# A graph-network layer: gathered features copied on ScalarE into the tile that TensorE reads

## The chip, the core and the metric

The kernel runs on one core of a Trainium2 chip. The core has five engines with instruction queues of their own: TensorE (PE, matrix products and transposes; its weight loads are shown apart as PEld), VectorE (DVE), ScalarE (ACT), GpSimd (POOL) and SyncE (SP). They work side by side and wait for one another through semaphores. The DMA engines move data between the chip's memory and the on-chip SBUF; TensorE writes into PSUM. The metric is the device time of one execution, in microseconds (us).

## What is computed

The layer passes messages along 212500 edges of a graph of 12500 nodes with 64 features each, sorted by their destination, and updates every node:

```python
msg_in     = concatenate([nodes[row], nodes[col], edge_features], axis=-1)   # 64 + 64 + 32
messages   = relu(msg_in @ mW1 + mb1) @ mW2 + mb2                            # hidden 128, out 64
aggregated = segment_sum(messages, col, num_segments=12500)
upd_in     = concatenate([nodes, aggregated], axis=-1)
out        = layernorm(x + relu(upd_in @ uW1 + ub1) @ uW2 + ub2)
```

`row` is an edge's source, `col` its destination. All of it is float32.

## The kernel before

The edges are cut into 554 groups of 384 (three tiles of 128 edges, an edge to a partition; the last group has 148). Because the edges are sorted by destination, the destinations of one group lie in a window of 32 consecutive nodes, whose first node is read from the data. A second, unordered version of the kernel stands behind a flag for inputs where this doesn't hold, and is not run here.

For each group g the tile `s` (128 partitions x 3 x 96 float32) holds for every edge 32 columns of a one-hot row (which of the window's nodes is its destination) and 64 columns of its source's features.

- `gather(g)` (L92 to L100): three indirect DMAs on POOL's queue fetch the 64 features of 128 source nodes each into columns 32 to 95 of `s`. The tile comes from a ring of 18 buffers (`AHEAD + 2`), and `gather(g + 16)` is called in iteration g.
- `onehot(g)` (L282 to L287): one DVE instruction compares the node numbers with 0 to 31 and writes columns 0 to 31 of the same `s`.
- `turn(g)` (L290 to L300): three TensorE transposes turn `s` into `xt` in PSUM (96 x 384, two buffers); one ACT instruction copies that into the tile `st` and sums the one-hot columns into `counts` (a second ACT instruction reads the sum out).
- `hidden(g)` (L302 to L315): three products of `st` (which also holds the 32 edge features, loaded by SP) with `wm`, a tile with the window's 32 rows of a per-node table and the weights; one ACT instruction applies relu into `h`.
- `sums(g)` (L317 to L326): a tiny transpose of the counts and three products of `h` with the one-hot columns of `s`, into `sg` in PSUM (two buffers).
- `add(g)` (L328 to L331): DVE adds `sg` to the running sums `agg`, and the counts to a row of `xc`.

`window` (SP) loads the 32 table rows of group g + 4, `inputs` (SP) loads the edge features of four groups at a time, `tables_for` makes the per-node table in 25 chunks ahead of its use, and `step_update` runs the node update of a finished chunk of 512 nodes in four steps, one step to an iteration.

The order of the instructions in each queue is written out by hand: each engine takes its own in the order of the program's calls, and the framework puts in the semaphore waits. The main loop's order in iteration g is

```python
gather(g + AHEAD); tables_for(g + SOON); window(g + NEXT)
onehot(g + 2); turn(g + 1); hidden(g)
sg = sums(g - 2); step_update(g - 2); add(g - 2, sg)
```

So in iteration g TensorE runs the transposes of g + 1, the `pre` products of g and the `sg` products of g - 2; ACT runs the copy to `st` of g + 1 and the relu of g; DVE runs the one-hot of g + 2 and, behind it, the addition of g - 2. An `s` buffer is given back when the `sg` products of its group are done.

Of the kernel before, what the change touches and what calls it, by code (L numbers as in the profile page):

```python
# [10 lines left out]
F32 = mybir.dt.float32  # L11
BF16 = mybir.dt.bfloat16
I32 = mybir.dt.int32
AF = mybir.ActivationFunctionType
# [5 lines left out]
P = 128  # L20
N = 12500
E = 212500
D = 64
# [5 lines left out]
W = 32  # L29
TG = 3  # L30
# [11 lines left out]
def tiles_of(g):  # L42

    n = min(GE, E - g * GE)
    return [min(P, n - j * P) for j in range((n + P - 1) // P)]


def plan():
# [22 lines left out]
def ordered(ctx: ExitStack, tc: tile.TileContext, a, ok):  # L71
# [3 lines left out]
    nc = tc.nc  # L75
    x, out = a["x"], a["out"]
    const = ctx.enter_context(tc.tile_pool(name="const", bufs=1))
    dram = ctx.enter_context(tc.tile_pool(name="dram", bufs=1, space=DRAM))
    gp = ctx.enter_context(tc.tile_pool(name="gather", bufs=AHEAD + 2))
# [11 lines left out]
    gathered = {}  # L91

    def gather(g):
        s = gp.tile([P, TG, W + D], F32, name="s")
        for j, p in enumerate(tiles_of(g)):
            t = g * TG + j
            nc.gpsimd.indirect_dma_start(  # L97
                out=s[:p, j, W:], out_offset=None, in_=x[:, :],
                in_offset=bass.IndirectOffsetOnAxis(ap=src_sb[:p, t : t + 1], axis=0),
            )  # L100
        gathered[g] = s
# [7 lines left out]
    for g in range(AHEAD):  # L109
        gather(g)  # L110
# [7 lines left out]
    iota = iop.tile([P, W], F32, name="iota")  # L118
# [72 lines left out]
    def tables_for(g):  # L191

        while tables and tables[0][3] <= g:
            table()
# [51 lines left out]

    early.close()
    ep = ctx.enter_context(tc.tile_pool(name="edge", bufs=3))
    up = ctx.enter_context(tc.tile_pool(name="upd", bufs=2))
    xtp = ctx.enter_context(tc.tile_pool(name="xt_ps", bufs=2, space=PSUM))  # L250
    prp = ctx.enter_context(tc.tile_pool(name="pre_ps", bufs=2, space=PSUM))
    sgp = ctx.enter_context(tc.tile_pool(name="sg_ps", bufs=2, space=PSUM))
    counts = const.tile([D + W, G], F32, name="counts")

    st, starts, hs = {}, {}, {}

    def inputs(b):
        if b * SB >= G:
            return
        c0, c1 = b * SB * GE, min(E, (b + 1) * SB * GE)  # L260
        t = stp.tile([P, SB * GE], F32, name="st")
        nc.sync.dma_start(t[D + W :, : c1 - c0], a["efT"][:, c0:c1])
        st[b] = t

    def columns(g):
        t, c = st[g // SB], (g % SB) * GE
        return t, c, sum(tiles_of(g))

    def window(g):
        if g >= G:  # L270
            return
        if g % SB == 0:
            n = min(SB, G - g)
            _, v = nc.values_load_multi_w_load_instructions(
                start_i[0:1, g : g + n], engines=[ET.SP, ET.DVE], min_val=0, max_val=N - 1,
                skip_runtime_bounds_check_because="they were clamped to the nodes on the chip",
            )
            for i in range(n):
                starts[g + i] = v[i]
        nc.sync.dma_start(wm[g % NW][:W, :], by_dst[bass.ds(starts[g], W), :])  # L280

    def onehot(g):  # L282
        if g >= G:
            return
        nc.vector.tensor_tensor(  # L285
            gathered[g][:, :, :W], iota.unsqueeze(1).to_broadcast([P, TG, W]),
            dlc[:, g * TG : (g + 1) * TG].unsqueeze(2).to_broadcast([P, TG, W]), ALU.is_equal,  # L287
        )

    def turn(g):  # L290

        if g >= G:
            return
        s = gathered[g]
        t, c, n = columns(g)
        xt = xtp.tile([D + W, GE], F32, name="xt")
        for j, p in enumerate(tiles_of(g)):
            nc.tensor.transpose(xt[:, j * P : j * P + p], s[:p, j, :], ident[:p, :p])  # L298
        nc.scalar.activation(t[: D + W, c : c + n], xt[:, :n], AF.Copy,  # L299
                             accum_out=counts[:, g : g + 1])  # L300

    def hidden(g):  # L302
        t, c, n = columns(g)
        sizes = tiles_of(g)
        pre = prp.tile([P, TG, H], F32, name="pre")
        for j, p in enumerate(sizes):
            nc.tensor.matmul(pre[:p, j, :], t[:, c + j * P : c + j * P + p], wm[g % NW],  # L307
                             start=True, stop=True)
        h = ep.tile([P, TG, H], F32, name="h")
        if len(set(sizes)) == 1:  # L310
            nc.scalar.activation(h, pre, AF.Relu)  # L311
        else:
            for j, p in enumerate(sizes):
                nc.scalar.activation(h[:p, j, :], pre[:p, j, :], AF.Relu)
        hs[g] = h  # L315

    def sums(g):  # L317
        h, s = hs.pop(g), gathered.pop(g)
        sizes = tiles_of(g)
        sg = sgp.tile([P, TIMES + 1, W], F32, name="sg")  # L320
        nc.tensor.transpose(sg[0:1, TIMES, :], counts[:W, g : g + 1], ident[:W, :W])  # L321
        for j, p in enumerate(sizes):
            nc.tensor.matmul(sg[:, :TIMES, :], h[:p, j, :],  # L323
                             s[:p, j, :W].unsqueeze(1).to_broadcast([p, TIMES, W]),
                             start=j == 0, stop=j == len(sizes) - 1)
        return sg  # L326

    def add(g, sg):  # L328
        at = bass.ds(starts.pop(g), W)
        nc.vector.tensor_tensor(agg[:, at], sg[:, 0, :], agg[:, at], ALU.add)  # L330
        nc.vector.tensor_tensor(xc[0:1, at], sg[0:1, TIMES, :], xc[0:1, at], ALU.add)  # L331
# [53 lines left out]
    def step_update(g):  # L385

        nonlocal now
        if not now and waiting and waiting[0][0] <= g:
            steps = waiting.pop(0)[1]
            now = [steps[0](), *steps[1:]]  # L390
        elif now:
            got = now[1](now[0])
            now = [got, *now[2:]] if len(now) > 2 else []
# [2 lines left out]
    inputs(1)  # L396
    for g in range(NEXT):
        window(g)
    onehot(0)
    onehot(1)  # L400
    turn(0)
    for g in range(G + 2):
        if g < G:
            if g % SB == 0:
                inputs(g // SB + 2)
            if g + AHEAD < G:
                gather(g + AHEAD)
            tables_for(g + SOON)
            window(g + NEXT)
            onehot(g + 2)  # L410
            turn(g + 1)
            hidden(g)
        if g > 1:
            sg = sums(g - 2)
            step_update(g - 2)
            add(g - 2, sg)
# [284 lines left out]
@with_exitstack  # L701
def gnn_layer(ctx: ExitStack, tc: tile.TileContext, a):
    nc = tc.nc
    flag = ctx.enter_context(tc.tile_pool(name="flag", bufs=1))
    ok = flag.tile([1, 1], I32, name="ok")
    with tc.manual_schedule():
        ordered(tc, a, ok)
    good = nc.values_load(ok[0:1, 0:1], min_val=0, max_val=1,
                          skip_runtime_bounds_check_because="a comparison's result")
    with tc.If(good == 0):  # L710
        with tc.manual_schedule():
            unordered(tc, a)
# [35 lines left out]
```

## Time and profile before

Three runs took 2529.65, 2532.01 and 2534.0 us, median 2532.01. The profiled execution took 2528.93 us; its span, from the first to the last instruction, is 2527.2 us, so 1.7 us lie outside it, and it stands 3 us under the median.

| what | before |
|---|---|
| profiled execution | 2528.93 us |
| span | 2527.2 us |
| TensorE busy (9359 matmul records) | 1697.3 us, 67% |
| POOL busy (1661 indirect DMAs) | 1570.3 us, 62% |
| ACT busy | 598.2 us, 24% |
| DVE busy | 392.9 us, 16% |
| mean granted TensorE clock | 0.786 |

The span over 554 groups is 4.56 us a group. In the lists of groups a row gives the line, the engine, the operation, output and inputs, the shapes, the number of instructions, their busy time and mean duration in ns, and then the idle time of the engine just ahead of them with what ended it. `remote` stands for a release that the trace does not tie to an instruction, `issue` for idle time in which no wait is seen. The duration of a TensorE record is modelled; when its semaphore really arrives is seen at the instruction that waits for it.

### The profile page before, as it was taken

How to read it: one execution, taken by the hardware profiler on the slowest of the kernel's cores; microseconds unless marked ns; L12 is line 12 of the kernel's file. 1: busy time of each engine (PE TensorE's matmuls, PEld its weight loads, DVE VectorE, ACT ScalarE, POOL GpSimd, SP SyncE). 2: the span in 40 equal slices, each digit the busy share in tenths (PEclk: the TensorE clock that was granted, in tenths of full speed). 3: DMA queues.
4: the chain of work that ended last, by engine and by line, in shares of the span. 5: the costliest groups of instructions: out<-in, count | busy, mean ns of one | idle time of the engine just before them, and what ended most of it. 6: DMA issues, size and time to landing. Idle time of an engine off the chain costs nothing.

```text
span 2527.2 us, 31410 instructions
## 1 busy us (share of the span) xinstructions
PE 1697.3 (67%) x9359; PEld 1457.9 (58%) x9359; DVE 392.9 (16%) x2103; ACT 598.2 (24%) x1740; POOL 1570.3 (62%) x1668
## 2 busy tenths in 40 slices
PE   0566767776676776776666766666667676677667
PEld 0455656665565665665555655556566565666556
DVE  3111111111111111111111111111111111111112
ACT  0222222222222222222222222222222222222223
POOL 6666666666666666666666665666666666666661
PEclk9787777777778677777877787788787778787879
DMA  5111111111111111111111111111111111111111
GB/s 127 34 43 46 40 43 45 41 44 43 40 44 41 42 47 39 45 43 40 43 41 42 47 42 40 40 43 44 41 42 47 36 47 40 43 47 38 46 39 28
DMA packets 99895, 111.48 MB, mean 44 GB/s; under 512 B 39997, under 2 KB 65062, under 8 KB 99590
## 3 DMA queue, kind: packets, MB, share of 16 engines
q0 software_dynamic: 53152, 54.51, 9.6%
q1 hardware_dynamic: 41928, 45.07, 6.4%
q10 hardware_dynamic: 4638, 9.80, 1.3%
q8 instruction: 79, 1.29, 0.2%
q14 instruction: 98, 0.80, 0.1%
HBM read 99.55 MB, written 9.62 MB: 43 GB/s over the span
## 4 chain that ended last, share of the span: by engine, by line
PE 66%; another core or an unknown queue 16%; issue 12%; DVE 2%; ACT 1%; DVEq 0%; DMA 0%; ACTq 0%
PE sg L323 25%; PE pre L307 21%; PE xt L298 12%; PE sg L321 2%; PE u_ps L184 2%; PE u_ps L357 2%; PE u_ps L344 1%; PE u_ps L345 1%; ACT st L299 1%; DVE o L374 0%; DVE mv L364 0%; DVE stats L363 0%; DVE xc L331 0%; DVE y L359 0%
## 5 line engine op out<-in xcount | busy, mean ns | idle before, releaser
L97 POOL DMA_INDIRECT s<-in_x,src_sb x1661 | 1569.6, 945 | 910.3 <-issue 420.5
L307 PE MATMUL pre<-wm,st 128*128 128x128 f32 x3322 | 635.3, 343 | 205.1 <-issue 140.3
L307 PEld LDWEIGHTS pre<-wm,st 128*128 128x128 f32 x3322 | 572.1, 254 | 241.7 <-issue 165.3
L323 PE MATMUL sg<-s,h 128*128 128x128 f32 x3322 | 660.4, 348 | 1.8 <-issue 1.8
L298 PE MATMUL xt<-ident,s 128*96 128x128 f32 x1661 | 355.4, 335 | 443.8 <-remote 246.7
L323 PEld LDWEIGHTS sg<-s,h 128*128 128x128 f32 x3322 | 535.6, 240 | 29.2 <-issue 1.7
L298 PEld LDWEIGHTS xt<-ident,s 128*96 128x96 f32 x1661 | 234.3, 159 | 501.7 <-remote 259.2
L299 ACT ACTIVATE st<-xt 96x384 f32<-96x384 f32 x554 | 267.9, 484 | 1002.3 <-PE xt L298 469.4
L311 ACT ACTIVATE h<-pre 128x384 f32<-128x384 f32 x553 | 268.8, 486 | 668.0 <-PE pre L307 257.3
L330 DVE TENSOR_TENSOR agg<-sg,agg 128x32 f32 x554 | 106.2, 192 | 1899.2 <-PE sg L323 761.2
L285 DVE TENSOR_TENSOR s<-iota,dlc 128x96 f32<-128x96 f32 x554 | 141.9, 257 | 54.6 <-issue 53.7
L184 PE MATMUL u_ps<-w1b,xc 65*128 65x128 f32 (+1 forms) x196 | 54.2, 453 | 112.9 <-DVE xc L331 80.3
L184 PEld LDWEIGHTS u_ps<-w1b,xc 65*128 65x128 f32 (+1 forms) x196 | 47.5, 326 | 118.2 <-issue 51.9
L321 PE MATMUL sg<-ident,counts 32*1 32x32 f32 x554 | 107.2, 194 | 0.0
L299 ACT ACTIVATION_READ_ACCUMULATOR st<-xt 96x1 f32 x554 | 106.0, 191 | 0.0
L331 DVE TENSOR_TENSOR xc<-sg,xc 1x32 f32 x554 | 99.2, 179 | 13.9 <-PE u_ps L345 5.3
L321 PEld LDWEIGHTS sg<-ident,counts 32*1 32x1 f32 x554 | 41.1, 74 | 90.2 <-issue 43.9
L357 PE MATMUL u_ps<-u,u 128*128 128x64 f32 (+1 forms) x196 | 49.5, 399 | 20.5 <-issue 11.2
L357 PEld LDWEIGHTS u_ps<-u,u 128*128 128x128 f32 (+1 forms) x196 | 47.1, 324 | 23.2 <-issue 12.2
L344 PE MATMUL u_ps<-agg,wc 128*128 128x512 f32 (+1 forms) x50 | 33.3, 753 | 18.0 <-DVE agg L330 12.2
L187 ACT ACTIVATE t<-u_ps 128x512 f32<-128x512 f32 (+1 forms) x25 | 14.7, 588 | 91.3 <-issue 43.7
L366 ACT ACTIVATE rstd<-mv,eps 128x4 f32<-128x4 f32 (+1 forms) x25 | 7.4, 297 | 103.8 <-DVE mv L364 42.1
(51 smaller groups left out, 188.1 us busy)
## 6 DMA issues: line engine op xcount, KB each, us to landing
s<-in_x,src_sb POOLq DMA_INDIRECT x1661
st<-in_efT SPq DMA_DIRECT2D x138, 192.0 KB
wm<-by_dst SPq DMA_DIRECT2D x554, 16.0 KB
by_dst<-t ACTq DMA_DIRECT2D x24, 256.0 KB
xin<-in_x SPq DMA_DIRECT2D x24, 128.0 KB
out<-o SPq DMA_DIRECT2D x24, 128.0 KB
xc<-in_xT ACTq DMA_DIRECT2D x1, 1589.0 KB
xc<-in_xT ACTq DMA_DIRECT2D x1, 1152.0 KB
```

Source lines behind the costliest of these rows:

```text
L97: nc.gpsimd.indirect_dma_start(out=s[:p, j, W:], out_offset=None, in_=x[:, :], in_offset=bass.IndirectOffsetOnAxis(ap=src_sb[:p, t : t + 1 ...
L184: nc.tensor.matmul(ps[:p, k], xc[:, base + k : base + p * n : n], w1b, start=True, stop=True)
L285: nc.vector.tensor_tensor(gathered[g][:, :, :W], iota.unsqueeze(1).to_broadcast([P, TG, W]), dlc[:, g * TG : (g + 1) * TG].unsqueeze(2).to ...
L298: nc.tensor.transpose(xt[:, j * P : j * P + p], s[:p, j, :], ident[:p, :p])
L299: nc.scalar.activation(t[: D + W, c : c + n], xt[:, :n], AF.Copy, accum_out=counts[:, g : g + 1])
L307: nc.tensor.matmul(pre[:p, j, :], t[:, c + j * P : c + j * P + p], wm[g % NW], start=True, stop=True)
L311: nc.scalar.activation(h, pre, AF.Relu)
L321: nc.tensor.transpose(sg[0:1, TIMES, :], counts[:W, g : g + 1], ident[:W, :W])
L323: nc.tensor.matmul(sg[:, :TIMES, :], h[:p, j, :], s[:p, j, :W].unsqueeze(1).to_broadcast([p, TIMES, W]), start=j == 0, stop=j == len(sizes ...
L330: nc.vector.tensor_tensor(agg[:, at], sg[:, 0, :], agg[:, at], ALU.add)
L331: nc.vector.tensor_tensor(xc[0:1, at], sg[0:1, TIMES, :], xc[0:1, at], ALU.add)
L357: nc.tensor.matmul(o_ps[:p, k], u[:, k:q:n], u2, start=True, stop=True)
```

## The change

The gathered rows get a tile of their own, `s` (128 x 3 x 64), in the same ring of 18. A new tile `wx` (128 x 3 x 96, a ring of 6) takes the place of the old `s`: DVE writes the one-hot columns into it, and ACT copies the gathered 64 columns beside them, in one instruction for a full group. Transposes and `sg` products read `wx`. `onehot` becomes `collect`, called at the same places, so in ACT's queue the copy of group g + 2 stands ahead of the copy to `st` of g + 1 and the relu of g. A buffer of `s` is given back when the ACT copy is done.

```diff
+def runs(sizes):
+    if len(set(sizes)) == 1:
+        return [(0, len(sizes), sizes[0])]
+    return [(j, 1, p) for j, p in enumerate(sizes)]
...
     def gather(g):
-        s = gp.tile([P, TG, W + D], F32, name="s")
+        s = gp.tile([P, TG, D], F32, name="s")
...
-                out=s[:p, j, W:], out_offset=None, in_=x[:, :],
+                out=s[:p, j, :], out_offset=None, in_=x[:, :],
...
+    wxp = ctx.enter_context(tc.tile_pool(name="wx", bufs=6))
...
-    def onehot(g):
+    def collect(g):
+
         if g >= G:
             return
+        t, s = wxp.tile([P, TG, W + D], F32, name="wx"), gathered.pop(g)
         nc.vector.tensor_tensor(
-            gathered[g][:, :, :W], iota.unsqueeze(1).to_broadcast([P, TG, W]),
+            t[:, :, :W], iota.unsqueeze(1).to_broadcast([P, TG, W]),
             dlc[:, g * TG : (g + 1) * TG].unsqueeze(2).to_broadcast([P, TG, W]), ALU.is_equal,
         )
+        for j, m, p in runs(tiles_of(g)):
+            nc.scalar.activation(t[:p, j : j + m, W:], s[:p, j : j + m, :], AF.Copy)
+        wx[g] = t
 
     def turn(g):
...
-        s = gathered[g]
+        s = wx[g]
...
     def sums(g):
-        h, s = hs.pop(g), gathered.pop(g)
+        h, s = hs.pop(g), wx.pop(g)
...
-            onehot(g + 2)
+            collect(g + 2)
             turn(g + 1)
             hidden(g)
```

More of the change, by code (lines that the diff above doesn't have):

```diff
@@ L253, in ordered @@
     counts = const.tile([D + W, G], F32, name="counts")
-    st, starts, hs = {}, {}, {}
+    st, starts, hs, wx = {}, {}, {}, {}
     def inputs(b):
@@ L398, in ordered @@
         window(g)
-    onehot(0)
-    onehot(1)
+    collect(0)
+    collect(1)
     turn(0)
```

## The prediction

> **What bounds the kernel now.** I read the page's list of groups first, to see which engine is near the span. (A row: line, engine, operation, tiles, shapes, count | busy us, mean ns | idle ahead of it, and its releaser.)
>
> ```profile
> span 2527.2 us, 31410 instructions
> PE 1697.3 (67%) x9359; PEld 1457.9 (58%) x9359; DVE 392.9 (16%) x2103; ACT 598.2 (24%) x1740; POOL 1570.3 (62%) x1668
> ...
> L97 POOL DMA_INDIRECT s<-in_x,src_sb x1661 | 1569.6, 945 | 910.3 <-issue 420.5
> ...
> L311 ACT ACTIVATE h<-pre 128x384 f32<-128x384 f32 x553 | 268.8, 486 | 668.0 <-PE pre L307 257.3
> L330 DVE TENSOR_TENSOR agg<-sg,agg 128x32 f32 x554 | 106.2, 192 | 1899.2 <-PE sg L323 761.2
> ```
>
> No engine is full. POOL needs 1569.6 us for its gathers and 420.5 us of issue gaps between them, 1990.1 us; the other 489.8 us of its idle time (910.3 less 420.5) are waits, nearly all for a free `s` buffer. So POOL is held back by the loop. DVE and ACT sit idle and wait for TensorE, and TensorE is idle a third of the time. This is a ring of waits, not a full engine.
>
> Next I read the waits, to see where TensorE stands still.
>
> ```profile
> POOL s L97 <- DVE agg L330: 301.7, 152, 8.2
> ...
> PE xt L298 <- remote: 246.7, 73, 6.2
> PE pre L307 <- issue: 140.3, 83, 3.7
> PE xt L298 <- PE sg L323: 107.2, 89, 2.2
> PE xt L298 <- issue: 89.4, 41, 23.1
> ...
> PE pre L307 <- ACT st L299: 64.6, 28, 12.0
> ```
>
> (Total us, times, longest.) The transposes wait 203 times (73, 89, 41) for 443 us together, the `pre` products 111 times (83, 28) for 205 us. Their real releasers are in the timeline: `xt` starts right behind a one-hot, `pre` right behind an ACT copy to `st`. I count these 314 waits as the places where a later one-hot or a later `st` can show.
>
> Then the timeline of a stretch in the middle and one at the end, where all gathers are done.
>
> ```profile
> 1003.60 0.19 DVE L330 TENSOR_TENSOR agg<-sg,agg 128x32 f32 x1 [4.82 <-PE pre L307]
> ...
> 1003.86 0.26 DVE L285 TENSOR_TENSOR s<-iota,dlc 128x96 f32<-128x96 f32 x1
> ...
> 1003.96 0.48 ACT L299 ACTIVATE st<-xt 96x384 f32<-96x384 f32 x1
> ...
> 1008.46 0.94 PE L323 MATMUL sg<-s,h 128*128 128x128 f32 x6
> ...
> 1016.73 0.19 DVE L330 TENSOR_TENSOR agg<-sg,agg 128x32 f32 x1 [4.95 <-PE sg L323]
> ```
>
> ```profile
> 2488.23 0.94 PE L323 MATMUL sg<-s,h 128*128 128x128 f32 x6
> ...
> 2489.21 0.19 DVE L330 TENSOR_TENSOR agg<-sg,agg 128x32 f32 x1 [1.46 <-PE sg L323]
> ...
> 2489.53 0.49 ACT L299 ACTIVATE st<-xt 96x384 f32<-96x384 f32 x1 [0.76 <-PE xt L298]
> ```
>
> At the end an addition starts 0.04 us behind its products. In the middle the products recorded at 1008.46 to 1009.40 are not added until 1016.73, though DVE stands idle for 4.95 us ahead of that: the completion reaches the waiting engine 7 us late. The windows table, cut to the additions (busy us, their count, the granted clock, DMA share, GB/s), says how much that matters:
>
> ```profile
> 1000.00:1040.00 40.00, 1.53 (x8) 0.75 0.18 48
> ...
> 2482.00:2502.00 20.00, 1.92 (x10) 1.00 0.11 30
> ```
>
> 8 groups in 40 us while POOL gathers, 10 in 20 us once it has stopped (at 2481 us): 2 us a group against 4.56 on average. So the loop is paced by late completions of TensorE while gathers run, and by the answers that follow each of them: `agg`, `xc`, one-hot on DVE, then `xt`; `st` on ACT, then `pre`. Why they are late the trace doesn't say.
>
> **The change part by part.**
>
> *The copies.* 553 full groups and two pieces of the last: 555 ACT instructions. No row has an ACT copy from SBUF of this size. By shape, the relu of 128x128 takes 277 ns and that of 128x384 486 ns; these are the ends, and a straight line through them gives 277 + 64 x 0.816 = 329 ns at 192 columns, which I take. ACT grows by 555 x 0.329 = 183 us to 781 us, 31% of the span, and stays far from full. At the end of the kernel, where a group takes 1.98 us, ACT has `st` 0.49, its read-out 0.19 and the relu 0.49: 1.17 us, and 1.50 with the copy. It still fits, so that stretch keeps its pace.
>
> *What now waits for the copy.* The transposes of a group needed its one-hot; now they need the copy, which itself waits for the one-hot (same tile). That puts 0.33 us and one more hand-over (0.04 us, as at 2489.21) behind the one-hot: 0.37 us at each of 203 waits, 75 us if every one shows.
>
> *What is queued behind the copy.* ACT takes its queue in order: behind the copy of g + 2 stand `st` of g + 1 and the relu of g. The copy waits for the one-hot of g + 2, which DVE runs behind the addition of g - 3. So `st` of g + 1 now waits for an addition that it had nothing to do with. In the burst at 1003.60 the one-hot ends at 1004.12, 0.52 us behind the start of the addition; the copy would end at 0.52 + 0.04 + 0.33 = 0.89 us, and `st` started at 0.36. That is 0.53 us later, at each of 111 `pre` waits: 59 us if every one shows. The relu comes later by as much, but its `h` is used two iterations on. In 25 chunks of the update DVE also has the normalization in that queue; I count that in the upper end.
>
> *How much shows.* All: 75 + 59 = 134 us. None: 0, if the late completions set the pace and 0.4 to 0.5 us disappear in lags of several us. The trace speaks for both: TensorE's dispatch does stand still at those places, but what it then issues is often reported late again. I take half, 67 us, and keep both ends.
>
> *The ring of gathers.* A buffer is now free after the copy of its group (iteration k - 2), not after its `sg` products (iteration k + 2), so gathers can run four groups further ahead. POOL's 489.8 us of waiting do not come off the time, as TensorE, not data, is late: gathers are issued 16 groups, some 73 us, ahead of use. The gain is at the end: four more groups are left when POOL stops, at 1.98 instead of 4.56 us, 10 us. It is also where POOL now waits 7.87 us once at 87 us; the two are one gain. If POOL itself became late, the next wait would be the copy's, for the gather.
>
> *What goes.* The transposes' waits for three gathers go to the copy. They cost nothing now, being 73 us old, and cost nothing there. The one-hot's wait becomes one for the copy of six groups before, equally old. The three indirect DMAs of a group keep number, size and order; POOL's issue gap of about 0.3 us stays. SP's instructions are the same; a later `st` can delay an edge-feature load and the window loads behind it, which run four groups (18 us) ahead: 0, and 0.5 us a group if that cover were gone.
>
> *Does it matter which tile TensorE reads?* The row first: 5 us a group with gathers in flight, 2 us without, so something of the gathers reaches TensorE. If it were that TensorE reads a tile that DMAs write into, the change would remove it. The Trainium skill, page "SBUF — State Buffer", section "Who interferes with whom", says that DMA uses ports of its own and that TensorE and ScalarE wait for no one; by it the new tile gains nothing, and by it the 2 and 5 us should not differ at all. This trace contradicts the second half. The sum here takes 0 for it, and rival three has the other end.
>
> *Sum.* 67 - 10 = 57 us on the profiled 2529, that is 2586; the median of the runs stands 3 us higher: 2532 + 57 = 2589 us.
>
> **The rivals.** One: all of it is hidden. Late completions cover the copy, the 10 us at the end remain: 2522 us. For it: lags of 3 to 7 us against 0.4. Against it: TensorE idles at just the places where the chain grows.
>
> Two: all shows, and groups that don't wait today begin to. 134 - 10 gives 2656; if the `st` delay also shows in a quarter of the other 443 groups, 111 x 0.53 = 59 us more, 2715. For it: the copy ties `st` to DVE's queue in every group.
>
> Three, the other side: gathers stop disturbing TensorE, because it no longer reads a tile that they write or because they run in one stretch far ahead. Then completions come as at the end of the trace, and POOL is the bound: 1661 x (0.945 + 0.30) = 2068 us, 3 us ahead of it, 20 groups at 1.98 = 40 and 25 us of last updates: 2136 us, 2141 as a median. It decides as soon as completions come within 0.1 us in the middle too; half of it gives some 2340. Against it: gathers write the same bytes at the same rate.
>
> **How the numbers follow.** A measurement here tells a change from none at about 0.2%, 2527 to 2537. My forecast, 2537 to 2656, has 0.52; rival two, above 2656, 0.16; rival one, 2515 to 2537, 0.18, of which 0.10 is below 2527; rival three, below 2515, 0.14. Faster 0.10 + 0.14 = 0.24, same 0.08, slower 0.52 + 0.16 = 0.68. The range leaves out most of rival three and what of rival two is above 2715, 0.2 together: 2505 to 2715. The forecast's own range is 2537 to 2656.
>
> **What would show it.** In the profile after: 555 ACT copies near 329 ns; TensorE's `xt` waits now ended by the copy and longer by some 0.4 us; `st` starting behind a copy; POOL's waits ended by ACT; ten or more groups at 2 us each behind the last gather, some 20 of them. The forecast is wrong if additions follow their products at once while POOL runs (rival three), or if the waits grow and the span doesn't (rival one). It is also wrong if the copy takes nearer 486 ns, which adds half of 0.16 x 314 = 25 us.

## The result, and the profile after

The changed kernel takes 2683.31 us (median of four runs, 2676.83 to 2693.18), the kernel before, run beside it, 2533.01 us. The ratio is 1.0585, with a 95% interval of 1.0561 to 1.0609: 5.9% slower. The forecast was 2589 us with a range of 2505 to 2715. The sign and the range hold; of the growth, 150 us, the forecast had 57.

The profiled execution took 2676.83 us, its span is 2675.1 us, 148 us longer than before. The mean granted clock of TensorE is 0.765 (before 0.786). First the page of after: the busy time of each engine, and the groups that answer to those shown of before, with the new copy (busy us, mean ns | idle ahead of it, what ended most of it).

```profile
span 2675.1 us, 32393 instructions
PE 1678.5 (63%) x9359; PEld 1432.0 (54%) x9359; DVE 373.0 (14%) x2103; ACT 733.0 (27%) x2295; POOL 1574.3 (59%) x1668
...
L104 POOL DMA_INDIRECT s<-in_x,src_sb x1661 | 1573.5, 947 | 1042.5 <-ACT wx L300 557.1
...
L324 ACT ACTIVATE h<-pre 128x384 f32<-128x384 f32 x553 | 269.3, 487 | 497.3 <-PE pre L320 176.3
L343 DVE TENSOR_TENSOR agg<-sg,agg 128x32 f32 x554 | 107.9, 195 | 2086.9 <-remote 966.4
L300 ACT ACTIVATE wx<-s 128x192 f32<-128x192 f32 x555 | 196.6, 355 | 48.0 <-DVE ok L248 36.2
```

No engine does markedly more, except ACT, which stays far from full. What grew is idle time, on TensorE and on POOL alike. POOL's row is the one to look at: 1573.5 us of gathers, as before, and 1042.5 us of idle ahead of them where it was 910.3. The waits view of after (us in total, times, longest) splits this idle time.

```profile
POOL s L104 <- ACT wx L300: 557.1, 183, 7.0
POOL s L104 <- issue: 448.5, 1437, 2.4
PE xt L311 <- DVE agg L343: 165.0, 37, 10.1
PE pre L320 <- issue: 160.4, 85, 6.7
...
PE pre L320 <- ACT st L312: 108.4, 47, 3.8
...
PE xt L311 <- ACT wx L300: 51.0, 26, 7.3
```

Issue gaps are 448.5 us (before 420.5), the rest of POOL's idle time 594.0 us (before 489.8), nearly all of it a wait for a buffer that the copy gives back. Along POOL's queue the 148 us are thus: gathers 4, issue gaps 28, waits 104, and 12 us more outside the gathers' busy and idle time (before 2527.2 - 1569.6 - 910.3 = 47.3, after 59.1). TensorE names the copy for 51 us only.

The timeline of after shows how such a wait ends (start, length, engine, line, operation; in brackets the engine's idle time ahead).

```profile
1073.13 0.49 ACT L324 ACTIVATE h<-pre 128x384 f32<-128x384 f32 x1 [3.02 <-PE sg L336]
1073.52 0.35 ACT L300 ACTIVATE wx<-s 128x192 f32<-128x192 f32 x1
1073.85 0.19 DVE L343 TENSOR_TENSOR agg<-sg,agg 128x32 f32 x1 [6.01 <-PE sg L336]
1073.90 0.49 ACT L312 ACTIVATE st<-xt 96x384 f32<-96x384 f32 x1
...
1074.14 0.94 POOL L104 DMA_INDIRECT s<-in_x,src_sb  x1 [2.21 <-ACT wx L300]
1074.44 0.26 DVE L295 TENSOR_TENSOR wx<-iota,dlc 128x96 f32<-128x96 f32 x1 [0.28 <-issue]
```

In before, in the stretch that the prediction shows, a wait ended like this:

```profile
1003.57 0.49 ACT L311 ACTIVATE h<-pre 128x384 f32<-128x384 f32 x1 [2.33 <-PE pre L307]
...
1003.83 0.94 POOL L97 DMA_INDIRECT s<-in_x,src_sb  x1 [2.19 <-DVE agg L330]
```

Two things are to be seen. After the change POOL starts again 1.01 us after the relu that was first to hear of TensorE, because the copy that frees the buffer stands behind that relu; in before it was 0.26 us behind the relu, and 0.23 us behind the addition of 1003.60 that was released with it. The gather of 1074.14 starts 0.27 us behind the end of the copy, and I counted the same distance, between 0.2 and 0.3 us, at 194 of the 203 stops of after (a stop is an idle time of POOL of over 0.7 us between two gathers). The second thing: the copy of 1073.52 writes the columns beside those of the one-hot of 1074.44, which is of the same group: it did not wait for it. Of the 554 groups, 364 have their copy start ahead of their one-hot.

Last the windows of after, cut to the additions of L343 (busy us, count, granted clock, DMA share, GB/s), a stretch with gathers and one after the last, which ends at 2617.6 us:

```profile
1000.00:1040.00 40.00, 1.52 (x8) 0.79 0.16 35
...
2620.00:2640.00 20.00, 1.92 (x10) 1.00 0.14 40
```

A group takes 2 us at the end, as before, and 23 additions lie behind the last gather, where 17 did.

### The profile page after: what moved, and what is told of

Same layout as the page of the kernel before. It is cut to its first block, busy times and chain, and to the rows that moved or that the text cites. A ratio compares the mean times of both kernels' runs of the same rounds, so it can differ in the third digit from the quotient of the medians.

```text
span 2675.1 us, 32393 instructions
## 1 busy us (share of the span) xinstructions
PE 1678.5 (63%) x9359; PEld 1432.0 (54%) x9359; DVE 373.0 (14%) x2103; ACT 733.0 (27%) x2295; POOL 1574.3 (59%) x1668
## 4 chain that ended last, share of the span: by engine, by line
PE 43%; another core or an unknown queue 24%; issue 18%; POOL 7%; DVE 4%; ACT 2%; DMA 1%; DVEq 0%; ACTq 0%; SPq 0%; POOLq 0%
PE sg L336 15%; PE pre L320 15%; PE xt L311 7%; POOL s L104 7%; PE u_ps L191 2%; PE sg L334 2%; PE u_ps L357 1%; PE u_ps L358 1%; ACT st L312 1%; ACT wx L300 1%; DMA xc<-ones 1%; DVE xc L344 1%; DVE agg L343 1%; PE u_ps L370 1%
## 5 line engine op out<-in xcount | busy, mean ns | idle before, releaser
L104 POOL DMA_INDIRECT s<-in_x,src_sb x1661 | 1573.5, 947 | 1042.5 <-ACT wx L300 557.1
L320 PE MATMUL pre<-wm,st 128*128 128x128 f32 x3322 | 627.9, 340 | 269.0 <-issue 160.4
L320 PEld LDWEIGHTS pre<-wm,st 128*128 128x128 f32 x3322 | 559.2, 249 | 317.6 <-issue 185.7
L311 PE MATMUL xt<-ident,wx 128*96 128x128 f32 x1661 | 350.7, 331 | 570.3 <-DVE agg L343 165.0
L336 PE MATMUL sg<-wx,h 128*128 128x128 f32 x3322 | 647.5, 343 | 0.0
L311 PEld LDWEIGHTS xt<-ident,wx 128*96 128x96 f32 x1661 | 232.0, 157 | 625.3 <-issue 451.7
L336 PEld LDWEIGHTS sg<-wx,h 128*128 128x128 f32 x3322 | 525.6, 236 | 27.1
L343 DVE TENSOR_TENSOR agg<-sg,agg 128x32 f32 x554 | 107.9, 195 | 2086.9 <-remote 966.4
L300 ACT ACTIVATE wx<-s 128x192 f32<-128x192 f32 x555 | 196.6, 355 | 48.0 <-DVE ok L248 36.2
L295 DVE TENSOR_TENSOR wx<-iota,dlc 128x96 f32<-128x96 f32 x554 | 133.7, 242 | 38.5 <-issue 27.4
```

Source lines behind the costliest of these rows:

```text
L104: nc.gpsimd.indirect_dma_start(out=s[:p, j, :], out_offset=None, in_=x[:, :], in_offset=bass.IndirectOffsetOnAxis(ap=src_sb[:p, t : t + 1] ...
L295: nc.vector.tensor_tensor(t[:, :, :W], iota.unsqueeze(1).to_broadcast([P, TG, W]), dlc[:, g * TG : (g + 1) * TG].unsqueeze(2).to_broadcast ...
L300: nc.scalar.activation(t[:p, j : j + m, W:], s[:p, j : j + m, :], AF.Copy)
L336: nc.tensor.matmul(sg[:, :TIMES, :], h[:p, j, :], s[:p, j, :W].unsqueeze(1).to_broadcast([p, TIMES, W]), start=j == 0, stop=j == len(sizes ...
```

## The experiments

The expectations speak of theories by letters. R, formed from the two traces, looks for the loss in the release of a buffer: POOL has to wait for TensorE, then for ACT's queue, then for the copy. S, formed after e1 to e4, is the theory of taking turns: while gathers run, TensorE gets almost nothing done, so POOL runs until no buffer is free, TensorE works while POOL stands still, and the time is the gathering plus all the stops. The letters C and Q look for the loss in the chain of answers on ACT's queue, as the prediction did. A is the load on ACT in e1 and e7, and how far gathers run ahead in e14 and e17; each text says what would follow.

For every kernel I counted POOL's stops in its trace. "Answer" is the mean time to POOL's next gather from the first instruction of ACT or DVE that follows over 1 us of idleness of its engine and starts in the stop or in the 0.3 us ahead of it. If only the stop itself is searched, the answers come out up to 0.3 us shorter, in nearly the same order.

| kernel | ratio (95%) | span us | stops | mean us | sum us | answer us |
|---|---|---|---|---|---|---|
| before | 1 | 2527.2 | 238 | 1.99 | 474 | 0.80 |
| e14, before, ring of 22 | 1.0011 (0.9995 to 1.0026) | 2522.4 | 229 | 1.96 | 450 | 0.71 |
| e16, before, one-hot earlier | 1.0001 (0.9983 to 1.0020) | 2520.0 | 239 | 1.92 | 460 | 0.69 |
| e10, before, pairs | 1.0093 (1.0063 to 1.0123) | 2569.9 | 212 | 2.38 | 504 | 1.04 |
| e1, before, unread copy | 1.0198 (1.0178 to 1.0218) | 2568.5 | 208 | 2.39 | 497 | 1.18 |
| e11, before, release through ACT | 1.0256 (1.0231 to 1.0281) | 2602.1 | 207 | 2.56 | 531 | 1.32 |
| e15, after, copy behind st | 1.0471 (1.0427 to 1.0516) | 2636.9 | 203 | 2.74 | 557 | 1.84 |
| e17, after, ring of 14 | 1.0493 (1.0457 to 1.0530) | 2631.6 | 197 | 2.83 | 558 | 1.64 |
| e12, after, collected earlier | 1.0574 (1.0544 to 1.0603) | 2678.4 | 204 | 2.92 | 596 | 1.90 |
| after | 1.0585 (1.0561 to 1.0609) | 2675.1 | 203 | 2.94 | 596 | 1.85 |
| e4, after, two copies | 1.0591 (1.0571 to 1.0611) | 2666.1 | 188 | 3.10 | 582 | 2.03 |
| e13, after again | 1.0628 (1.0601 to 1.0655) | 2712.4 | 198 | 3.20 | 633 | 2.06 |

The spans come from four sets of runs, on chips where before took 2533 (after), 2519 (e1, e4; e14 to e17) and 2541 us (e10 to e13). What is left of the span without the stops is 2053 to 2084 us in every row: 1661 gathers with the short gaps behind them, some 1.21 us each, and 49 to 67 us ahead of the first gather and behind the last. The rows stand in order of the ratio, and the mean stop and the answer rise with it nearly throughout. One more chip behaves otherwise: before takes 2108 us there, and the runs on it (e5, e6, e7, e9, e18, e19) are told of where that matters.

**Do gathers slow TensorE, whatever tile it reads?** In e2 all gathers but those of the first 16 groups go into a ring that nobody reads and that is free again at once; TensorE reads the 16 first tiles over and over. In e3 those gathers are left out. In both the features of later groups are those of the first 16.

```diff
 # e2
-        s = gp.tile([P, TG, W + D], F32, name="s")
+        s = (gp if g < AHEAD else sink).tile([P, TG, W + D], F32, name="s" if g < AHEAD else "sunk")
...
-        s = gathered[g]
+        s = gathered[g % AHEAD]
 # e3: the same, and in gather(g)
+        if g >= AHEAD:
+            return
```

> The kernel before, leaving out the use of the gathers behind the first 16 groups: every later group reads the tiles of the first 16 again, and its gathers go into a ring of six tiles that nobody reads, so POOL never waits for TensorE. If gathers as such hold TensorE's completions back (theory R's ground): POOL runs without a stop to about 2080 us, TensorE does some 6 us a group beside it and 2 us a group after it, 2450 to 2520 us in all. If completions are late only because TensorE reads tiles that DMAs write into, or because POOL and TensorE wait for each other: TensorE is done after 1200 to 1400 us and the time is POOL's, 2080 to 2120 us.

> The same without any gather behind the first 16 groups (left out). Theory R's ground: every group takes about 2 us as at the end of the trace of before, 1180 to 1330 us with the node updates. If the loop itself makes the completions late: over 2000 us.

e2 took 3539.54 us, e3 1386.04 us (one run each; before took 2519 us). Neither theory had foreseen the first, and the second is a little above R's 1180 to 1330. The slices of e2's page (busy tenths of 40 equal slices) and two of its windows (columns: us, PE, PEld, DVE, ACT, POOL, granted clock, DMA share, GB/s) show what happens:

```profile
PE   1000001000000010000000000069999999999998
...
POOL 6777777777777777777777777700000000000000
```

```profile
1000.00:1100.00 100.00, 8.42 (x32) 6.44 (x32) 0.94 (x6) 2.13 (x6) 75.41 (x72) 0.50 0.11 26
2500.00:2600.00 100.00, 97.14 (x710) 88.36 (x709) 26.35 (x154) 46.96 (x132) 0.00 (x0) 0.95 0.13 37
```

With nothing to stop POOL, TensorE almost stands still for 2300 us: 64 instructions in 100 us (32 matmuls, 32 weight loads) beside 72 gathers. Between 200 and 2200 us I counted 1432 matmuls and weight loads beside 1433 gathers, one to a gather, and 43 finished groups, one in 46 us. Behind the last gather the other 507 additions take 1219 us, 2.4 us each. It happens with tiles that no gather writes into. So it is the gathers themselves that hold TensorE back, and the 2100 us that the gathers alone would need are out of reach as long as TensorE's work has to wait for their end. Without them TensorE is the bound, at 92% busy:

```profile
span 1384.3 us, 28710 instructions
...
PE 1269.9 (92%) x9359; PEld 1143.9 (83%) x9359; DVE 375.1 (27%) x2103; ACT 621.3 (45%) x1740; POOL 49.0 (4%) x55
```

This turns the picture of before round. POOL's waits for a buffer are not slack: where POOL never waits, TensorE almost stands still. A stop begins when no buffer is free and ends when one is given back, and whatever lies between TensorE's completion and the next gather makes it longer.

S is too strong, though, where it has TensorE work only while POOL stands still. Take the starts of the relu, of the copy to `st` and of the addition as TensorE's answers, as each of them waits for TensorE. Between the 49th gather and the last, 488 of 1614 answers of before fall into a stop, and 1126 beside gathers. In the 111 stretches of before in which POOL gathers for at least 10 us, the answers start at 1.24 per us in the first 2 us, then at 0.69, 0.47 and 0.44 in the next three steps of 2 us, and at 0.25 from 8 to 10 us; at the end, without gathers, three answers in 1.98 us make 1.5 per us. TensorE is not short of instructions meanwhile: in these stretches its matmuls and weight loads start at 9 to 11 per us up to the 6th us, and at 5 per us behind it. So TensorE's answers thin out the longer POOL gathers without a stop, and e2 shows where that leads.

**The copy without its reader, and a second copy.** e1 is the kernel before with the 555 copies at the place that the change gives them, into a tile that nobody reads. e4 is the changed kernel with a second, unread copy behind the first.

```diff
 # e1, in onehot(g)
+        for j, m, p in runs(tiles_of(g)):
+            nc.scalar.activation(unread[:p, j : j + m, :], gathered[g][:p, j : j + m, W:], AF.Copy)
 # e4, in collect(g), behind the copy
+            nc.scalar.activation(unread[:p, j : j + m, :], s[:p, j : j + m, :], AF.Copy)
```

> The kernel before, with the same 555 ACT copies at the same place in ACT's queue, but into a tile that nobody reads; TensorE goes on reading the gathered tile, and a gather buffer is still given back by the sg products. Theory R (release): what costs is that POOL now waits for TensorE, then for ACT's queue, then for the copy, before it may gather on; here that path is as before, so 2525 to 2550 us. Rival A (load): the extra work and blocking in ACT's queue costs; then 2640 to 2690 us, as with the change.

> The changed kernel with the copy done twice, the second into a tile that nobody reads, so that a gather buffer is free one copy (0.35 us) later. Theory R: 204 restarts of POOL each 0.26 to 0.35 us later, 50 to 70 us more, 2730 to 2755 us. If the copy is not on the path that sets the time: 2683 within 15 us.

e1: ratio 1.0198 (1.0178 to 1.0218), about a third of the loss and between the two forecasts, R's 2525 to 2550 us and A's 2640 to 2690. It cannot be put down to the work in ACT's queue, since the way of giving a buffer back did not stay as it was. In e1 a buffer has a reader on ACT too, and POOL starts again later:

```profile
1050.08 0.19 DVE L340 TENSOR_TENSOR agg<-sg,agg 128x32 f32 x1 [5.86 <-PE sg L333]
...
1050.80 0.94 POOL L104 DMA_INDIRECT s<-in_x,src_sb  x1 [2.59 <-issue]
```

This is 0.72 us behind the addition that was released with it, where before had 0.23. In the records of POOL's queue the wait for TensorE is now an instruction of its own ahead of the gather, which itself waits for ACT; it ends 0.70 to 0.75 us ahead of the gather in 194 of the 208 stops of e1, and in 73 of the 208 no ACT instruction ends in that time. So this delay is POOL's own, and e1 has no price for the load on ACT alone.

e4: 1.0591 (1.0571 to 1.0611), as the change with one copy, where 50 to 70 us more were expected. By the words of its expectation that is the result of a copy that is not on the path that sets the time. The stops do become longer (3.10 us, the answer 2.03), but there are fewer of them, 188, and POOL gathers longer between two of them, 2.94 groups on average where it is 2.72 in after and 2.32 in before. That TensorE finishes more groups in a longer stop is the explanation that fits; it was found after the run and not tested. Length and number work against each other, so a price per stop cannot simply be multiplied by the stops of before.

**The release alone.** e5 is the kernel before, in which one column of `s` is also read by a tiny ACT instruction behind the `sg` products, in ACT's queue behind the relu, so that the buffer should come back through ACT. It was run twice, the second time as e11.

```diff
 # in sums(g), behind the sg products
+        nc.scalar.activation(unread[: sizes[0], :], s[: sizes[0], 0, W : W + 1], AF.Copy)
```

> The kernel before, with one ACT copy of a single column of s put into ACT's queue behind the relu of g, where the sg products of g - 2 are issued. TensorE reads what it read; only the giving back of a gather buffer now waits for ACT too. Theory S (stops): TensorE gets on only around POOL's stops, so the time is POOL's gathering plus its stops, and a stop is worth less the longer POOL gathers in between; a later release makes stops longer and fewer, so 1.0 to 3.5% slower than before. Rival C (chain): only the copy ahead of the transposes and of st costs; then within 0.5% of before.

> As before: the kernel before with a buffer given back through ACT's queue. If before takes about 2110 us here: within 0.5%. If it takes about 2520 us, theory S: 1.0 to 3.5% slower; rival C: within 0.5%.

e5 fell on the chip where before takes 2108 us and made no difference there (0.9996, 0.9986 to 1.0005). e11: 1.0256 (1.0231 to 1.0281), the answer 1.32 us. The waits of e11 seem to name the chain:

```profile
POOL s L97 <- ACT st L300: 298.0, 115, 3.5
POOL s L97 <- ACT unread L327: 115.8, 41, 7.0
```

In before 301.7 us of POOL's waits were put down to an addition that was merely released together with POOL; now they are put down to ACT instructions. The timeline shows that these are not the cause either:

```profile
1009.56 0.19 DVE L332 TENSOR_TENSOR agg<-sg,agg 128x32 f32 x1 [8.60 <-remote]
...
1009.66 0.49 ACT L300 ACTIVATE st<-xt 96x384 f32<-96x384 f32 x1 [6.65 <-remote]
...
1010.28 0.94 POOL L97 DMA_INDIRECT s<-in_x,src_sb  x1 [2.71 <-ACT st L300]
...
1010.51 0.19 ACT L327 ACTIVATE unread<-s 128x1 f32<-128x1 f32 x1
```

POOL starts again 0.72 us behind the addition, as in e1, and ahead of the tiny read of that iteration. The wait for TensorE in POOL's queue ends 0.70 to 0.80 us ahead of the gather in 187 of the 207 stops; in 49 of the 207 no ACT instruction ends in the last 0.72 us. The `st` copy with its read-out, which hears of TensorE in the same moment, happens to end shortly before. So S's 1.0 to 3.5% holds in number and not by the way that was meant: the buffer does not come back by way of the relu, but POOL needs 0.5 us more in a stop to get going once it has one more thing to wait for. TensorE reads the same tiles in the same order; ACT has 554 tiny instructions of 0.19 us more, whose part was not tested by itself. A later start of POOL after each stop goes with a loss of 64 us. That is more than the whole 57 us of the forecast, in a place where the forecast had nothing.

**The chain of answers.** e6 is the changed kernel with `collect(g + 4)` for `collect(g + 2)`, with 8 buffers of `wx`: copy and one-hot are then done well ahead of the transposes. e12 is the same kernel again.

```diff
-    wxp = ctx.enter_context(tc.tile_pool(name="wx", bufs=6))
+    wxp = ctx.enter_context(tc.tile_pool(name="wx", bufs=8))
...
-            collect(g + 2)
+            collect(g + 4)
```

> The changed kernel with one-hot and copy of a group made two iterations earlier (g + 4, a ring of 8 tiles). The copy is no longer just ahead of the transposes that need it, but it stands in the same place in ACT's queue and a gather buffer is still given back by it. Theory S: 4.5 to 6% slower than before, as the change. Rival C: most of the loss goes, 1 to 3% slower.

> As before: the changed kernel with one-hot and copy two iterations earlier. If before takes about 2110 us here: 0.2 to 0.6% slower. If it takes about 2520 us, theory S: 4.5 to 6% slower, as the change; rival C: 1 to 3% slower.

e6, on the chip of 2108 us: 1.0037 (1.0025 to 1.0050). e12: 1.0574 (1.0544 to 1.0603), beside e13, the changed kernel unaltered on the same chip, 1.0628 (1.0601 to 1.0655).

> The changed kernel itself, beside the three others. If before takes about 2110 us here, POOL's gathering sets the time and the copy is hidden: within 0.7% of before. If it takes about 2520 us: 5.6 to 6.1% slower, as measured.

Half a percent comes back: S's 4.5 to 6% holds, C's 1 to 3% is missed, and e13 lies a little above the 5.6 to 6.1% expected. TensorE's groups in e12, below those of after, tell why this is the clearest run against the prediction's sum:

```profile
L320 PE MATMUL pre<-wm,st 128*128 128x128 f32 x3322 | 627.9, 340 | 269.0 <-issue 160.4 <-ACT st L312 108.4
L311 PE MATMUL xt<-ident,wx 128*96 128x128 f32 x1661 | 350.7, 331 | 570.3 <-DVE agg L343 165.0 <-remote 117.2 <-DVE wx L295 82.0
```

```profile
L320 PE MATMUL pre<-wm,st 128*128 128x128 f32 x3322 | 641.9, 345 | 833.5 <-ACT st L312 496.5 <-issue 323.1 <-ACT wx L300 13.4
L311 PE MATMUL xt<-ident,wx 128*96 128x128 f32 x1661 | 332.1, 318 | 27.8 <-issue 27.8
```

The transposes' waits have gone from 570.3 us to 27.8, and the `pre` products have them instead, 833.5 for 269.0 us. Where TensorE is seen to wait is a matter of which instruction is next while gathers hold it; taking one such wait away moves it to the next instruction.

e9, run again as e16, does the same to the kernel before: `onehot(g + 4)` for `onehot(g + 2)`.

```diff
-            onehot(g + 2)
+            onehot(g + 4)
```

> The kernel before with the one-hot made two iterations earlier (g + 4), so that the transposes never wait for DVE. If the 203 waits of the transposes for a one-hot (443 us) are time that counts: 2 to 6% faster than before. If they only mark time in which TensorE is held back anyway: within 1% of before.

> The kernel before with the one-hot called two groups earlier (g + 4 instead of g + 2), so that the transposes never wait for DVE's queue. If the chain of addition, one-hot and transposes counts in the stops: 1 to 3% faster. Theory S: a stop ends with the sg products, whatever the one-hot does, within 1% of before. On a chip where before takes about 2108 us, both within 0.7%.

e9, on the chip of 2108 us: 0.9994 (0.9984 to 1.0004). e16: 1.0001 (0.9983 to 1.0020), within S's 1%. The one-hot's place behind the addition does not set the time either.

**How far gathers run ahead.** e7 gives the kernel before one tile of `s` for two groups, so that buffers come back in pairs; run again as e10. e14 gives it 22 buffers for 18, e17 gives the changed kernel 14, which takes back the four groups of its earlier release.

```diff
 # e7, e10
-    gp = ctx.enter_context(tc.tile_pool(name="gather", bufs=AHEAD + 2))
+    gp = ctx.enter_context(tc.tile_pool(name="gather", bufs=AHEAD // 2 + 1))
...
+        if g % 2 == 0:
+            pair[:] = [gp.tile([P, 2, TG, W + D], F32, name="s")]
+        s = pair[0][:, g % 2]
 # e14: bufs=AHEAD + 6    e17 (changed kernel): bufs=AHEAD - 2
```

> The kernel before with one s tile for two groups (a ring of 9), so that buffers come free in pairs and POOL gathers two or four groups in a stretch; nothing else changes, ACT has no copy. Theory S: stretches grow from 2.3 to about 2.9 groups, stops get fewer, 3 to 7% slower. Rival C, and rival A (ACT's load): within 0.5% of before.

> As for the pairs before: the kernel before with one s tile for two groups. If before takes about 2110 us here, POOL never stops and this is within 0.5% again. If before takes about 2520 us, theory S: fewer and longer stretches of gathering, 3 to 7% slower. Rivals C and A: within 0.5%.

> The kernel before with 22 instead of 18 buffers of s, given back at the same place as before: gathers may run four groups further ahead, as the change lets them. Theory S (gathering and TensorE's work take turns, and the change costs what each stop of the gathers becomes longer, because the buffer comes back through the relu and the copy): how far ahead makes no difference, within 0.5% of before. Rival A (the change costs because gathers run further ahead): 3 to 6% slower. On a chip where before takes about 2108 us, both within 0.7%.

> The kernel after with 14 instead of 18 buffers of s, which takes back the four groups that the earlier give-back lets gathers run ahead. Theory S: as after, 5.3 to 6.5% slower than before. Rival A (further ahead is what costs): within 1.5% of before. On a chip where before takes about 2108 us, both within 0.7%.

e7, on the chip of 2108 us: 1.0000 (0.9991 to 1.0010). e10: 1.0093 (1.0063 to 1.0123), where S had expected 3 to 7%: a stop has to wait for two groups, but there are fewer stops (212), again the trade that e4 showed. e14: 1.0011 (0.9995 to 1.0026); running further ahead costs and brings nothing, and A falls. e17: 1.0493 (1.0457 to 1.0530), below S's 5.3 to 6.5% and far from A's 1.5%; most of the loss stays with the run-ahead taken away.

**The place in ACT's queue.** e15 is the changed kernel with the one-hot alone in `collect(g + 2)`, and the copy, now `copy(g + 2)`, behind the copy to `st` and ahead of the relu.

```diff
             collect(g + 2)
             turn(g + 1)
+            copy(g + 2)
             hidden(g)
```

> The kernel after with the copy of g + 2 in ACT's queue behind the copy to st of g + 1 and ahead of the relu of g, instead of ahead of both. Theory S: a stop no longer ends with a relu (0.49 us) and a copy (0.36 us) but with an st copy (0.49 us) and a copy, so the stops keep about their length: 5 to 6.5% slower than before, as after; if a stop gets shorter by the relu's 0.49 us at 200 stops, 98 us come back and it is some 2% slower. Rival Q (the loss is the delay of st behind the copy, the prediction's 0.53 us): that delay is gone, 1 to 3% slower. The two are told apart only by the length of the stops in the trace: S wants it to fall with the time. On a chip where before takes about 2108 us, both within 0.7%.

1.0471 (1.0427 to 1.0516). Q's 1 to 3% is missed: the delay of `st` is gone and most of the loss is there. S's first number is just missed too. The copy now ends a stop behind `st` and its read-out instead of behind the relu, and the answer takes as long, 1.84 us for 1.85. Two more runs were to show on one chip whether the order brings back the 1% by which e15 is under after:

> The changed kernel itself, on the same chip as the next run, since the order in ACT's queue was tried on a chip on which the changed kernel had not run. As measured elsewhere: 5.6 to 6.6% slower than before (on a chip where before takes about 2108 us: within 0.7%).

> The copy of g + 2 behind the copy to st of g + 1, beside the changed kernel on the same chip. If that order takes something back, this is 0.7 to 1.7% faster than the changed kernel, and the mean stop of the gathers is 0.1 to 0.4 us shorter; if the 4.7% of its first run were the chip's, the two agree within 0.4%.

Both fell on the chip of 2108 us, and both took 1.0007 (0.9998 to 1.0016). The 1% of the order, and that of e17, stay open. But e18 is the changed kernel on a chip that does not hold TensorE, and its page and waits are worth a look:

```profile
span 2107.2 us, 32393 instructions
...
PE 1545.8 (73%) x9359; PEld 1269.3 (60%) x9359; DVE 374.1 (18%) x2103; ACT 710.4 (34%) x2295; POOL 1573.0 (75%) x1668
...
L104 POOL DMA_INDIRECT s<-in_x,src_sb x1661 | 1572.2, 947 | 514.4 <-issue 394.1
L311 PE MATMUL xt<-ident,wx 128*96 128x128 f32 x1661 | 322.6, 308 | 485.4 <-ACT wx L300 457.0
```

```profile
POOL s L104 <- issue: 394.1, 1293, 0.3
POOL s L104 <- DMA s<-in_x,src_sb: 106.7, 327, 3.1
...
POOL s L104 <- ACT wx L300: 0.9, 3, 0.3
```

POOL stops 5 times in all, its waits for the copy are 0.9 us where they were 557.1, and TensorE has time to spare: it waits 457.0 us for copies that wait for gathers. POOL is the bound, and the same change costs 0.07%, with an interval that includes no change at all. The 6% therefore appears only where gathers hold TensorE and POOL stops; the copy's work and the longer way through ACT's queue are there on this chip too, and cost nothing that can be measured.

No variant beat the kernel before.

## Why the prediction was wrong in size

*Reading the bound.* "This is a ring of waits, not a full engine" holds, and so does the 2 us a group without gathers. That TensorE's completions come late while gathers run was read off the trace correctly. What was not asked is what this makes of POOL's waits. That the range held the measured time was luck: the way there was another.

*"The ring of gathers"* is the step that failed. It set POOL's 489.8 us of waiting aside, "as TensorE, not data, is late". e2, e11 and e18 show that on the chips where the loss appears they are part of the time. They grew by 104 us, and the issue gaps by 28, together 132 of the 148 us. The step saw that a buffer comes back at another place and counted only that it is an earlier group; that the new place is behind a relu and a copy, while POOL stands waiting, had no price. By the timelines it was 1.01 us for 0.26, on the mean of all stops 1.85 for 0.80, and 194 of the 203 stops end right behind a copy. The mean stop grew by 0.95 us, which over after's 203 stops is 193 us, less what 35 stops fewer save (35 x 1.99 = 70): some 122 us, the difference of the sums in the table split in two. That 35 stops fewer would come with longer ones could not be had from the trace of before, and e4 shows that the size does not follow from the length of a stop alone.

*"What now waits for the copy"* took the tile as the unit of waiting: the copy was to wait for the one-hot of its tile. The columns are apart, and 364 of 554 copies start first. Its 75 us had a second fault: e12 takes those waits away and saves 0.5%.

*"What is queued behind the copy"* forecast 59 us at the `pre` products, whose waits went from 205.1 to 269.0, by 64 us. The match means little: in e12 they are 833.5 us at nearly the time of after. Its 0.53 us also rested on the copy waiting for the one-hot, and so for the addition; as two copies in three don't, little more than the copy's own 0.36 us is left there. What the longer ACT queue costs by itself stays open, since in e1 POOL's start is later by 0.5 us too, as in e11, and e1 loses no more than that run.

*"How much shows"*: half of a sum whose terms both lay in waits that do not set the time, as e12 and e16 show for the transposes and e15 for most of the rest. Rival two's span of 2656 to 2715 us holds the measured value, but its mechanism, every one of those waits showing, is not what happened.

*The copies* took 355 ns, not 329, and 196.6 us, not 183; this was of no weight. ACT's busy time grew by 135 us only, to 733 and not 781, as consecutive instructions overlap (the relu of 1073.13 ends at 1073.62, the copy starts at 1073.52). The Trainium skill, page "ScalarE: Activation LUTs", section "What ACT_TABLE_LOAD costs", gives 186 ns + 0.833 ns for each column with immediate scale and bias, by which I estimate 346 ns for 192 columns: nearer than the straight line through two relus that I used.

*The end.* 23 additions at 2 us each stood behind the last gather, as forecast (some 20), six more than before. It was booked as a gain of 10 us, since those groups would else have taken 4.56 us each. But if the gathers and their stops are the time, groups that are left over at the end are added to it; along POOL's queue that part is 12 us on the other side.

*Which tile TensorE reads* was costed at nothing, and rival three was to come true if it mattered. e2 settles it: TensorE is held while it reads tiles into which no gather writes. The half sentence that the gathers "write the same bytes at the same rate" was right. The Trainium skill's rule, page "SBUF — State Buffer", section "Who interferes with whom", that DMA never contends with a compute engine, speaks of the ports of SBUF. Taken as the prediction took it, that gathers leave TensorE's time as it is, it does not hold here: 46 us a group with gathers, 2.4 without. Whether the ports have a part in it no run shows.

## What to carry to other kernels

When two engines disturb each other, an engine that waits often and is far from full can still be the time: ask what the other one does during its waits, and follow the release of a buffer to the instruction that ends the wait, with all that stands ahead of that instruction in its queue. Where a wait only shows which instruction was next while something else held the engine, adding up such waits prices nothing; one run that removes the suspected disturber (here the gathers) shows this before anything is summed. And a price per stop has to be set against the number of stops, which changes with it. Last, read in the trace of a test whether it changed only what it was meant to: an added reader of a buffer also changed what the next writer waits for.

## What the runs showed of the hardware

- Indirect gathers in an unbroken row let TensorE issue one instruction per gather (1432 to 1433 in 2000 us of e2), while the same instructions take 2.4 us a group without them. What they share wasn't found: it is not the tile, and bytes moved were few (26 GB/s and a DMA share of 0.11 in that window, 37 GB/s and 0.13 where TensorE ran freely).
- The hold sets in over a stretch of gathering: in before TensorE's answers start at 1.24 per us in its first 2 us and at 0.25 from 8 to 10 us.
- POOL starts a gather 0.23 us behind the instruction that was released with it in before, and 0.72 us in e1 and e11, where ACT also reads the buffer. That the further wait in POOL's queue is the reason fits the records and was not tested by itself.
- Chips differ in this hold. On one, the same program takes 2108 us (before, in two sets of runs), POOL gathers almost without a stop, and TensorE keeps up with it; on those where before takes 2519 to 2541 us it doesn't. Why is open.
- The granted clock fell with the idling: 0.97 in e3, 0.79 in before, 0.77 in after, 0.50 in the held stretch of e2. It follows how busy TensorE is kept here, and no run shows it as the cause.
